# A two-layer graph network: exponentials of edge scores taken on ScalarE straight from a score row, weight sums and block ends moved from GpSimd to VectorE, and a new order of the first blocks

## The chip, the cores and the metric

The kernel runs on one NeuronCore of a Trainium2 chip. The metric is the device time of one execution in microseconds (us). Engines are called PE (TensorE), DVE (VectorE), ACT (ScalarE), POOL (GpSimd) and SP (SyncE, which only issues DMAs here).

## The reference

There are 1250 nodes with 1024 features and 41250 edges. The first layer normalises, runs a relational graph convolution with two relations, and adds its output back. The second layer is the one that the change touches:

```python
def _L1_gnn_ref(x, W, a, src, dst):
    h = x @ W                                    # 1250 x 1024 @ 1024 x 1024
    al, ar = h @ a[0, :d], h @ a[0, d:]
    e = jnp.exp(-jax.nn.leaky_relu(al[src] + ar[dst], negative_slope=0.1))
    rowsum = jax.ops.segment_sum(e, src, num_segments=N)
    h_prime = jax.ops.segment_sum(e[:, None] * h[dst], src, num_segments=N)
    return jax.nn.elu(h_prime / (rowsum[:, None] + 1e-5))

x = x + _L0_gnn_ref(relu(layernorm(x)), ...)
x = x + _L1_gnn_ref(relu(layernorm(x)), W, a, src, dst)
```

## The kernel before

Nodes are kept in T = 10 tiles of 128 (the last has 98). The edges have been turned into a dense matrix of counts between every two nodes, so the second layer is dense: the weight between source node i and destination node j is the count times exp of minus the leaky relu of the summed score. The scores are stored with their sign turned, so the weight before the count is the lesser of exp(z) and exp(0.1 z), where z is the score of i plus the score of j.

**The places where scores lie.** `scores(t)` (L871) copies the two scores of the nodes of tile t into `score`; `n_ar[:, t]` is then a column, one number for each partition (destination node). `row(t)` (L1037) turns the other score into a row that is the same in all partitions, `rows[:, t, :]`, by a PE transpose (L1040) and a DVE copy (L1041).

**One source tile s** (128 source nodes against all 10 tiles of destinations, 128 x 1280 numbers) goes through these steps:

- `add_scores(s)` (L1091, DVE): z = row + column, written by pieces of 4, 4 and 2 tiles (512, 512 and 256 columns).
- `exps(s)` (L1096 and L1097, ACT): exp(0.1 z) into a second buffer `tenth(s)`, exp(z) in place in `raw(s)`.
- `lesser(s)` (L1102, DVE), `times_counts(s)` (L1108, DVE): the lesser of the two, times the counts.
- `sum_weights(s)` (L1116 to L1128, POOL): adds the ten tiles into `zsum`, which `sum_rows(s)` (L1177, PE) sums over partitions; `inverse(s)` (L1182, L1183, DVE) follows.
- `high_parts(s)` (L1132, ACT), `low_parts(s)` (L1136, DVE), `differences(s)` (L1140, DVE): the weights split in a high and a low part h and l, and a combination m of both, so that three fast fp32r products give an fp32 product. The values of the nodes are split in the same way: `parts_of(t)` (L893 ACT, L894 DVE) and `third_form(engine, t)` (L1144).

**Blocks and their matmuls.** A block (s, c) is the 128 outputs of source tile s in half c of the 1024 columns. `multiply(s, c, "hl")` (L1165) is 20 matmuls of 512 columns; `scale(s, c)` (L1171, ACT) then multiplies the sum in PSUM by 4097; `multiply(s, c, "m")` is 10 more into the same sum. `elu_of(s, c)` (L1193 to L1196) and `put_out(s, c)` (L1201, L1202) scale by the inverse, apply the elu, add x, which `load_rest` (L1157) fetched, and store. The very last block uses `last_out` (L1209 to L1213) instead.

**Buffers.** For s of 2 and more, all s share one `raw` and one `tenth` buffer; h, l, m and `zsum` alternate between two sets. The weights of s = 0 and s = 1 for the first eight tiles of destinations (`exps(s, 0, T - 2)` and so on) are made early, while the last product of x and W (L986: seven half-size products for each pair of tiles, whose PSUM results ACT evacuates at L1001, L1012, L1023 and L1029) still runs. In that part the framework's scheduler chooses the order.

**Order.** From L1319 on, the order of PE, DVE, ACT and POOL is the order in which the program is written. A first part (L1322 to L1360) fills in the last two tiles (A = 8 to B = 10) of s = 0 and s = 1; six of the ten third forms are on POOL, four on DVE. Then the loop over s (L1362 to L1399) overlaps the products of s with making the weights of s + 1. In iteration s the PE runs (s, 0) "hl", (s-1, 1) "m", (s, 1) "hl" and (s, 0) "m": 60 matmuls.

Of the kernel before, what the change touches and what calls it, by code (L numbers as in the profile page):

```python
# [8 lines left out]
F32 = mybir.dt.float32  # L9
# [4 lines left out]
AF = mybir.ActivationFunctionType  # L14
ALU = mybir.AluOpType
# [12 lines left out]
T = 10  # L28
# [382 lines left out]
def fast_arm(tc, ctx, edges, firsts, w_root, conv_bias, wo, w_gat, a_gat, out,  # L411
# [443 lines left out]
    score = const.tile([128, 2, T], F32, name="score")  # L855
    nc.vector.memset(score, 0.0)
    n_al, n_ar = score[:, 0, :], score[:, 1, :]
    rows = meta[:, D + 2:D + 2 + T * 128].rearrange("p (t n) -> p t n", t=T)

    def three(name):  # L860
# [10 lines left out]
    def scores(t):  # L871

        n = ROWS[t]
        ends = hs[t].rearrange("p (h c) -> p h c", h=2)[:n, :, H]
        nc.vector.tensor_copy(score[:n, :, t], ends)

# [207 lines left out]
        for t0, t1 in zip(ends, ends[1:]):  # L1086
            yield t0, t1, [at(f, t0, t1) for f in forms]

    def add_scores(s, a=0, b=T):
        for t0, t1, (z,) in each(a, b, raw(s)):  # L1090
            nc.vector.tensor_tensor(z, rows[:, s:s + 1, :].to_broadcast([128, t1 - t0, 128]),  # L1091
                                    n_ar[:, t0:t1, None].to_broadcast([128, t1 - t0, 128]), ALU.add)

    def exps(s, a=0, b=T):
        for t0, t1, (z, y) in each(a, b, raw(s), tenth(s)):
            nc.scalar.activation(y, z, AF.Exp, scale=0.1)  # L1096
            nc.scalar.activation(z, z, AF.Exp)  # L1097

    def lesser(s, a=0, b=T):

# [6 lines left out]
            z = z.rearrange("p t (a j) -> p t a j", a=4)  # L1107
            nc.vector.tensor_tensor(z, z, counts[:, t0:t1], ALU.mult)  # L1108

    def sum_weights(s, first=True, rest=True):  # L1110

        z, total, add = raw(s), zsum[s % 2], nc.gpsimd.tensor_add
        if s < 2:
            if first:
                y = early[1].rearrange("p (t n) -> p t n", n=128)
                add(y[:, :4], at(z, 0, 4), at(z, 4, 8))  # L1116
                add(y[:, :2], y[:, :2], y[:, 2:4])
                add(total, y[:, 0], y[:, 1])
            if rest:
                for t in (8, 9):  # L1120
                    add(total, total, at(z, t, t + 1)[:, 0])
        else:
            y = by_dsts[s].bitcast(F32)[:, :HD].rearrange("p (t n) -> p t n", n=128)
            add(y[:, :4], z[0][2], z[1][2])  # L1124
            add(total, at(z, 8, 9)[:, 0], at(z, 9, 10)[:, 0])
            add(y[:, :2], y[:, :2], y[:, 2:4])
            add(y[:, 0], y[:, 0], y[:, 1])
            add(total, total, y[:, 0])  # L1128

    def high_parts(s, a=0, b=T):  # L1130
        for t0, t1, (z, h) in each(a, b, raw(s), sets[s % 2]["h"]):
# [51 lines left out]
        nc.vector.reciprocal(inv[:n], inv[:n])  # L1183

    def buffers(s, c):
        return ends[3 * c:3 * c + 3]

    def elu_of(s, c):

        n = ROWS[s]  # L1190
        r, e, x = (v[:n] for v in buffers(s, c))
        v = sums_of[s, c][:n]
        nc.scalar.activation(e, v, AF.Exp, scale=invs[s][:n])  # L1193
        nc.scalar.activation(e, e, AF.Relu, bias=one[:n], scale=-1.0)
        nc.gpsimd.tensor_tensor(e, x, e, ALU.subtract)  # L1195
        nc.scalar.activation(r, v, AF.Relu, scale=invs[s][:n])  # L1196

    def put_out(s, c):
        n = ROWS[s]
        r, e, x = (v[:n] for v in buffers(s, c))  # L1200
        nc.vector.tensor_add(e, e, r)  # L1201
        nc.sync.dma_start(out[s * 128:s * 128 + n, c * HD:c * HD + HD], e)  # L1202

    def last_out(s, c):

        n = ROWS[s]
        r, e, x = (v[:n] for v in buffers(s, c))
        v = sums_of[s, c][:n]
        nc.scalar.activation(e, v, AF.Exp, scale=invs[s][:n])  # L1209
        nc.vector.tensor_scalar(r, v, invs[s][:n], 0.0, op0=ALU.mult, op1=ALU.max)  # L1210
        nc.vector.scalar_tensor_tensor(r, x, -1.0, r, op0=ALU.add, op1=ALU.add)
        nc.vector.scalar_tensor_tensor(e, e, 1.0, r, op0=ALU.min, op1=ALU.add)
        nc.sync.dma_start(out[s * 128:s * 128 + n, c * HD:c * HD + HD], e)  # L1213

    os_, oTs, hTs = {}, {}, {}
# [63 lines left out]
    for (i, j), after in zip(order, order[1:] + [None]):  # L1279
        p2(i, j)  # L1280
        p6(i, j)
        if j == 1 and i + 1 < T // 2:
            norm(2 * i + 2)
            turn_first(i + 1)
            norm(2 * i + 3)
        p5(i, j)
        p7(i, j)
        if after:
            p1(*after)
            if j == 1:  # L1290
                turn_second(i + 1)
        p4(i, j)
        p3(i, j)
        if j == 1:
            if after:
                rest_of_pair(i + 1)
            if after:
                for t in (2 * i, 2 * i + 1):
                    scores(t)
                for t in range(0 if i == 1 else 2 * i, 2 * i + 2):  # L1300
                    parts_of(t)
                for t in range(0 if i == 1 else 2 * i, 2 * i + 2):
                    row(t)
            if i == T // 2 - 2:

                early += [big.tile([128, D + 2], F32, name="early", tag="x8")[:, :D], long_tile("early")[:, :D]]
                for s in range(2):
                    add_scores(s, 0, T - 2)
                    exps(s, 0, T - 2)
                    lesser(s, 0, T - 2)  # L1310
                    times_counts(s, 0, T - 2)
                    sum_weights(s, rest=False)
                    if s == 0:
                        high_parts(s, 0, T - 2)
                        low_parts(s, 0, T - 2)
# [3 lines left out]
    with tc.manual_schedule(  # L1319
            engines={mybir.EngineType.PE, mybir.EngineType.DVE, mybir.EngineType.Activation,  # L1320
                     mybir.EngineType.Pool}):
        for t in range(6):  # L1322
            third_form(nc.gpsimd, t)
        for c in range(2):
            open_block(0, c)
            load_rest(0, c)
        multiply(0, 0, "hl", 0, A)
        for t in (A, A + 1):
            scores(t)
        sets[1]["h"], sets[1]["l"] = [place(wide("zh", "wo4"))], [place(wide("zl", "h"))]  # L1330
        high_parts(1, 0, A)
        low_parts(1, 0, A)
        hhs[A] = work.tile([128, KD * 128], F32R, name="hh8", tag="hT", bufs=2)
        parts_of(A)
        hhs[A + 1] = big.tile([128, D + 2], F32R, name="hh9", tag="x9")
        parts_of(A + 1)
        multiply(0, 1, "hl", 0, A)
        for t in (A, A + 1):
            row(t)
        for s in range(2):  # L1340
            add_scores(s, A, B)
            exps(s, A, B)
        for s in range(2):
            lesser(s, A, B)
            times_counts(s, A, B)
            high_parts(s, A, B)
        for i in (1, 0):
            sets[i]["m"] = [place(work.tile([128, T * 128], F32R, name="zm", tag="z", bufs=2))]
        for s in range(2):
            low_parts(s, A, B)  # L1350
            sum_weights(s, first=False)
        hms[A] = work.tile([128, KD * 128], F32R, name="hm8", tag="hT", bufs=2)
        hms[A + 1] = big.tile([128, D + 2], F32R, name="hm9", tag="x8")
        differences(0)
        for t in range(6, T):
            third_form(nc.vector, t)
        open_block(1, 0)
        multiply(1, 0, "hl", 0, A)
        for s, c in ((0, 0), (0, 1), (1, 0)):
            multiply(s, c, "hl", A, B)  # L1360

        for s in range(T):  # L1362
            nxt = s + 1 if 2 <= s + 1 < T else None
            if s > 1:
                open_block(s, 0)
                multiply(s, 0, "hl")
            if s:
                scale(s - 1, 1)
            if nxt:
                add_scores(nxt)  # L1370
            if s:
                elu_of(s - 1, 0)
                load_rest(s, 0)
            if nxt:
                exps(nxt)
            if s > 1:
                put_out(s - 2, 1)
            if s:
                put_out(s - 1, 0)
            if nxt:  # L1380
                lesser(nxt)
                times_counts(nxt)
                sum_weights(nxt)
                high_parts(nxt)
            scale(s, 0)
            if nxt:
                low_parts(nxt)
            sum_rows(s)
            if s:
                multiply(s - 1, 1, "m")  # L1390
                open_block(s, 1)
                multiply(s, 1, "hl")
            multiply(s, 0, "m")
            inverse(s)
            if s:
                elu_of(s - 1, 1)
                load_rest(s, 1)
            if nxt or not s:
                differences(s + 1)  # L1399
        scale(T - 1, 1)  # L1400
        elu_of(T - 1, 0)
        multiply(T - 1, 1, "m")
        put_out(T - 2, 1)
        put_out(T - 1, 0)
        last_out(T - 1, 1)


@with_exitstack
# [149 lines left out]
```

## Time and profile before

| | before |
|---|---|
| time, median of 3 runs (lowest to highest) | 602.16 us (601.88 to 602.29) |
| time of the profiled execution | 602.22 us |
| its span, first to last instruction | 600.4 us |
| granted clock of the PE, mean of the span | 0.989 |
| busy: PE, DVE, ACT, POOL | 580.2, 429.7, 260.3, 120.7 us |
| start of (3, 0) "hl" on the PE | 489.55 us |
| last DMA issued (L1213) | 594.70 us |

Times in the profile are us from the start of the span. In a timeline, each line has the start, the time taken, the engine, the line of the kernel, the operation, its output and input, and how many were merged; the brackets give the idle time before it and who ended it. A wait is written as engine, line, the engine and line it waited for: sum in us, how often, the longest. In a chain of waits each line is the time at which a step of the chain starts and how long it lasts on the chain.

### The profile page before, as it was taken

Reading aid. Unit: us, or ns where it says so; the run is one execution under the profiler, and the core shown is the slowest. Engines: PE = TensorE matmul, PEld = TensorE weight load, DVE = VectorE, ACT = ScalarE, POOL = GpSimd, SP = SyncE. Lnnn points to the kernel's source line nnn. Section 1 sums busy time; section 2 is a strip of 40 time slices with the busy share of each in tenths; the row PEclk is TensorE's granted clock in tenths of the full one; section 3 lists DMA queues with packets and bytes.
Section 4 is the critical chain, followed back from the end, with each engine's and each line's share of the span. In section 5 each row is a group of like instructions: output and inputs, shape, how many; then the busy total and the mean of one; then the engine's idle time right before and its main releaser. Section 6 shows DMA issues by size and latency. Waiting matters only on the chain.

```text
span 600.4 us, 8407 instructions
## 1 busy us (share of the span) xinstructions
PE 580.2 (97%) x2848; PEld 420.9 (70%) x2848; DVE 429.7 (72%) x988; ACT 260.3 (43%) x516; POOL 120.7 (20%) x111
## 2 busy tenths in 40 slices
PE   8999999999999999999999999999996899999993
PEld 5666666666656767767766888888874788888872
DVE  5889887888772766469899734234669988888831
ACT  3666566665542000003412233324513866677632
POOL 5010000000000000000000000000293666667740
PEclk9999999999999999999999999999997999999997
DMA  8950111110108601100126700000000022222211
GB/s 282 345 138 2 37 35 37 35 29 7 29 0 258 197 37 55 51 36 36 70 86 186 219 10 1 0 2 1 18 19 0 35 87 84 90 91 71 71 66 64
DMA packets 21928, 43.80 MB, mean 73 GB/s; under 512 B 2638, under 2 KB 7886, under 8 KB 21876
## 3 DMA queue, kind: packets, MB, share of 16 engines
q1 hardware_dynamic: 20308, 38.05, 18.8%
q0 software_dynamic: 1424, 5.12, 4.5%
q8 instruction: 24, 0.39, 0.3%
q14 instruction: 28, 0.23, 0.1%
q10 hardware_dynamic: 144, 0.00, 0.0%
HBM read 24.53 MB, written 13.52 MB: 63 GB/s over the span
## 4 chain that ended last, share of the span: by engine, by line
PE 84%; DVE 5%; issue 5%; DMA 2%; ACT 2%; SPq 1%; POOL 0%; POOLq 0%; DVEq 0%; ACTq 0%
PE mm L721 17%; PE mm L986 12%; PE mm L798 12%; PE tp L1165 10%; PE mm L1165 7%; PE acc L521 7%; PE mm L844 6%; PE z L986 5%; PE mm L902 3%; DMA w<-in_w_cat_dram 2%; PE p L902 2%; PE tp L576 1%; DVE d L1091 1%; PE mm L845 1%; DVE hm L1144 1%
## 5 line engine op out<-in xcount | busy, mean ns | idle before, releaser
L721 PE MATMUL mm<-w,hT 128*128 128x429 f32 (+1 forms) x320 | 143.7, 535 | 1.2 <-DMA w<-in_w_cat_dram 1.1
L520 DVE TENSOR_SCALAR key<-meta 125x320 bf16<-125x320 f16 x330 | 85.1, 300 | 24.2 <-PE acc L521 12.2
L528 ACT ACTIVATE cnt<-acc 128x320 f32 x110 | 49.8, 453 | 70.0 <-PE acc L521 62.0
L521 PEld LDWEIGHTS <-lo 125*128 125x128 bf16 x330 | 40.5, 126 | 50.5 <-issue 36.8
L798 PE MATMUL mm<-y,cnt 128*128 128x286 bf16 (+3 forms) x600 | 75.2, 284 | 0.4 <-DVE y L614 0.4
L521 PE MATMUL acc<-key,lo 125*128 125x320 bf16 x330 | 72.2, 303 | 0.0
L798 PEld LDWEIGHTS <-cnt 128*128 128x128 f16 (+1 forms) x600 | 59.5, 99 | 14.7 <-issue 1.0
L721 PEld LDWEIGHTS mm<-w,hT 128*128 128x128 f32 (+1 forms) x320 | 51.4, 190 | 6.5 <-issue 5.1
L1116 POOL TENSOR_TENSOR early<-early 128x512 f32<-128x512 f32 x2 | 2.6, 1278 | 239.3 <-DVE early L1108 239.3
L986 PE MATMUL mm<-w,a 128*128 128x257 f32 (+3 forms) x192 | 44.9, 379 | 0.0
L986 PEld LDWEIGHTS mm<-w,a 128*128 128x128 f32 (+1 forms) x192 | 35.7, 187 | 5.8 <-ACT h L1012 0.4
L809 ACT ACTIVATE bias<-bias 128x286 f32<-128x286 f32 (+1 forms) x10 | 4.4, 442 | 80.2 <-DVE bias L808 80.2
L844 PE MATMUL mm<-wo,meta 128*128 128x512 f32 (+1 forms) x80 | 37.6, 592 | 0.0
L1165 PE MATMUL tp<-hm,zm 128*128 128x512 f32 (+1 forms) x120 | 30.3, 399 | 1.5 <-ACT tp L1171 1.5
L495 DVE TENSOR_TENSOR lo<-meta 125x768 bf16<-125x768 f16 x55 | 30.3, 551 | 0.1
L1091 DVE TENSOR_TENSOR d<-meta,score 128x512 f32<-128x512 f32 (+1 forms) x26 | 26.8, 1082 | 0.0
L1165 PEld LDWEIGHTS tp<-hm,zm 128*128 128x128 f32 (+1 forms) x120 | 21.6, 184 | 7.2 <-ACT tp L1171 1.9
L1124 POOL TENSOR_TENSOR d<-d,d 128x512 f32<-128x512 f32 x8 | 19.0, 2380 | 34.7 <-DVE d L1108 34.7
L587 POOL DMA_DIRECT2D x<-h x10 | 9.1, 909 | 83.7 <-ACT h L558 73.6
L1201 DVE TENSOR_TENSOR meta<-meta,d 128x512 f32<-128x512 f32 x9 | 12.7, 1410 | 16.7 <-POOL meta L1195 16.7
L1165 PE MATMUL tp<-hh,zh 128*128 128x512 f32 (+3 forms) x60 | 24.0, 401 | 0.0
L1165 PE MATMUL tp<-parts,zl 128*128 128x512 f32 (+3 forms) x60 | 23.9, 398 | 0.0
(213 smaller groups left out, 1143.5 us busy)
## 6 DMA issues: line engine op xcount, KB each, us to landing
x<-h POOLq DMA_DIRECT2D x9, 512.0 KB, 4.6
xd<-x SPq DMA_DIRECT2D x9, 512.0 KB, 2.6
x<-in_x_dram SPq DMA_DIRECT2D x8, 512.0 KB, 12.7
w<-in_L_gnn_W_dram SPq DMA_DIRECT2D x8, 512.0 KB, 7.5
w<-in_w_cat_dram SPq DMA_DIRECT2D x8, 429.0 KB, 10.3
squares<-cnt SPq DMA_DIRECT2D x10, 320.0 KB, 3.2
d<-squares SPq DMA_DIRECT2D x40, 80.0 KB, 2.0
d<-xd SPq DMA_DIRECT2D x9, 256.0 KB, 2.6
```

What stands on the lines that cost most here:

```text
L495: nc.vector.tensor_tensor(los[q // 2], iota_lo, lows[:, q:q + 2, :].rearrange("p q j -> p (q j)")[:, None, :].to_broadcast([PE_, 128, 2 * J]),
L520: nc.vector.tensor_scalar(key, iota_key, keys[:, q, j:j + 1], None, op0=ALU.is_equal)
L521: nc.tensor.matmul(acc[:, :2 * T * W], los[q // 2][:, :, (q % 2) * J + j], key, start=(j == 0), stop=(j == J - 1))
L528: nc.scalar.activation(cnt_w[:, :, bass.ds(b, W)], a3, AF.Copy)
L721: nc.tensor.matmul(pys[t][:ROWS[t], r, :F + HF], hTs[t][0][:, k, :ROWS[t]], wcat[k][:, r, :], start=(k == 0), stop=(k == KD - 1))
L798: nc.tensor.matmul(pm[:n, r, :f], cnt[:k, h, r, t * 128:t * 128 + n], ybs[h][:k, s, r, :f], start=(h == 0 and s == 0), stop=(h == T - 1 an ...
L844: nc.tensor.matmul(po[:n, c, :], oT[:, i, :n], wo_of[i][:, cs], start=(i == 0), stop=False)
L902: nc.tensor.matmul(o, hT[:, k, :n], wg[k][:, c0:c1], start=(k == 0), stop=(k == KD - 1))
L986: nc.tensor.matmul(o[:a.shape[2], :c1 - c0], a[:, k, :], b[k][:, c0:c1], start=(start and k == 0), stop=(k == KH - 1), skip_group_check=no ...
L1091: nc.vector.tensor_tensor(z, rows[:, s:s + 1, :].to_broadcast([128, t1 - t0, 128]), n_ar[:, t0:t1, None].to_broadcast([128, t1 - t0, 128]) ...
L1124: add(y[:, :4], z[0][2], z[1][2])
L1165: nc.tensor.matmul(sums_of[s, c][:n], at(sets[s % 2][f], t, t + 1)[:k, 0, :n], h[:k, c * HD:c * HD + HD], start=(t == 0 and f == "h"), sto ...
```

## The change

`add_scores` goes. `exps` reads the row itself and passes the column as the bias of the activation; a column serves one tile only, so each tile takes two instructions of 128 columns: exp(row + n_ar) and exp(0.1 row + tenths), where `tenths` is a new table with a tenth of `n_ar`, filled by one more small DVE instruction in `scores`. `sum_weights` becomes three or four DVE additions for each s; only the last two tiles of s = 0 and s = 1 are added on POOL (`sum_last`). `elu_of` loses its second Relu on ACT and its POOL subtraction; `put_out` takes two DVE instructions instead of one, and also serves the last block, whose x is loaded into another buffer. Two third forms stay on POOL, eight are on DVE. The first part and the first two turns of the loop are written out in a new order: all four blocks of s = 0 and 1 have their "hl" before `multiply(0, 0, "m")`, which follows the first `differences`. The loop starts at s = 2.

```diff
@@ scores
         nc.vector.tensor_copy(score[:n, :, t], ends)
+        nc.vector.tensor_scalar(tenths[:n, t:t + 1], ends[:, 1:2], 0.1, None, op0=ALU.mult)
@@ exps
-        for t0, t1, (z, y) in each(a, b, raw(s), tenth(s)):
-            nc.scalar.activation(y, z, AF.Exp, scale=0.1)
-            nc.scalar.activation(z, z, AF.Exp)
+        for t0, t1, forms in each(a, b, raw(s), tenth(s)):
+            for form, n, scale in zip(forms, (n_ar, tenths), (1.0, 0.1)):
+                for t in range(t0, t1):
+                    nc.scalar.activation(form[:, t - t0, :], rows[:, s, :], AF.Exp, bias=n[:, t:t + 1], scale=scale)
@@ sum_weights (the old body of POOL additions is removed)
+    def sum_weights(s):
+        z, y, add = raw(s), tenth(s)[0][2], nc.vector.tensor_add
+        n = T - 2 if s < 2 else T
+        add(y[:, :4], at(z, 0, 4), at(z, 4, 8))
+        if n == T:
+            add(y[:, :2], y[:, :2], at(z, 8, 10))
+        add(y[:, :2], y[:, :2], y[:, 2:4])
+        add(zsum[s % 2], y[:, 0], y[:, 1])
+    def sum_last(s):
+        for t in (T - 2, T - 1):
+            nc.gpsimd.tensor_add(zsum[s], zsum[s], at(raw(s), t, t + 1)[:, 0])
@@ buffers
-        return ends[3 * c:3 * c + 3]
+        r, e, x = ends[3 * c:3 * c + 3]
+        return r, e, slots[4][:, :HD] if (s, c) == (T - 1, 1) else x
@@ elu_of, put_out (last_out is removed)
         nc.scalar.activation(e, v, AF.Exp, scale=invs[s][:n])
-        nc.scalar.activation(e, e, AF.Relu, bias=one[:n], scale=-1.0)
-        nc.gpsimd.tensor_tensor(e, x, e, ALU.subtract)
         nc.scalar.activation(r, v, AF.Relu, scale=invs[s][:n])
...
-        nc.vector.tensor_add(e, e, r)
+        nc.vector.scalar_tensor_tensor(e, e, 1.0, x, op0=ALU.min, op1=ALU.add)
+        nc.vector.scalar_tensor_tensor(e, r, -1.0, e, op0=ALU.add, op1=ALU.add)
@@ the early weights of s = 0 and 1
-                    add_scores(s, 0, T - 2)
                     exps(s, 0, T - 2)
...
-                    sum_weights(s, rest=False)
+                    sum_weights(s)
@@ the first part, as it is after
+        for t in range(2):
+            third_form(nc.gpsimd, t)
         for c in range(2):
             open_block(0, c)
             load_rest(0, c)
         multiply(0, 0, "hl", 0, A)
         for t in (A, A + 1):
             scores(t)
...
+        for t in (A, A + 1):
+            row(t)
+        parts_of(A)
+        for s in range(2):
+            exps(s, A, B)
...
+        high_parts(1, 0, A)
+        multiply(0, 1, "hl", 0, A)
+        lesser(0, A, B)
+        times_counts(0, A, B)
+        high_parts(0, A, B)
+        low_parts(1, 0, A)
+        parts_of(A + 1)
+        low_parts(0, A, B)
+        lesser(1, A, B)
+        times_counts(1, A, B)
+        high_parts(1, A, B)
+        low_parts(1, A, B)
         open_block(1, 0)
         multiply(1, 0, "hl", 0, A)
         for s, c in ((0, 0), (0, 1), (1, 0)):
             multiply(s, c, "hl", A, B)
+        for s in range(2):
+            sum_last(s)
...
+        differences(0)
+        for t in range(2, T):
+            third_form(nc.vector, t)
+        exps(2)
+        for c in range(2):
+            scale(0, c)
+        scale(1, 0)
+        open_block(1, 1)
+        multiply(1, 1, "hl")
+        scale(1, 1)
+        differences(1)
+        sum_rows(0)
+        multiply(0, 0, "m")
+        inverse(0)
+        elu_of(0, 0)
+        multiply(0, 1, "m")
+        lesser(2)
+        times_counts(2)
+        high_parts(2)
+        low_parts(2)
+        elu_of(0, 1)
+        put_out(0, 0)
+        load_rest(1, 0)
+        sum_rows(1)
+        multiply(1, 0, "m")
+        inverse(1)
+        differences(2)
+        multiply(1, 1, "m")
@@ the loop, as it is after
+        for s in range(2, T):
+            more = s + 1 < T
+            open_block(s, 0)
+            multiply(s, 0, "hl")
+            if s > 2:
                 scale(s - 1, 1)
+            sum_weights(s)
+            elu_of(s - 1, 0)
+            if more:
+                exps(s + 1)
+            put_out(s - 2, 1)
+            load_rest(s - 1, 1)
+            put_out(s - 1, 0)
+            load_rest(s, 0)
+            if not more:
+                load_rest(s, 1)
+            if more:
+                lesser(s + 1)
+                times_counts(s + 1)
+                high_parts(s + 1)
             scale(s, 0)
+            if more:
+                low_parts(s + 1)
+            if s > 2:
+                multiply(s - 1, 1, "m")
+            open_block(s, 1)
+            multiply(s, 1, "hl")
             sum_rows(s)
             multiply(s, 0, "m")
+            if more:
+                differences(s + 1)
             inverse(s)
+            elu_of(s - 1, 1)
         scale(T - 1, 1)
         elu_of(T - 1, 0)
         multiply(T - 1, 1, "m")
         put_out(T - 2, 1)
         put_out(T - 1, 0)
-        last_out(T - 1, 1)
+        elu_of(T - 1, 1)
+        put_out(T - 1, 1)
```

More of the change, by code (lines that the diff above doesn't have):

```diff
@@ L857, in fast_arm @@
     n_al, n_ar = score[:, 0, :], score[:, 1, :]
+    tenths = const.tile([128, T], F32, name="tenths")
+    nc.vector.memset(tenths, 0.0)
     rows = meta[:, D + 2:D + 2 + T * 128].rearrange("p (t n) -> p t n", t=T)
@@ L1087, in each @@
             yield t0, t1, [at(f, t0, t1) for f in forms]
[L1089 to L1092, printed above, removed]
     def exps(s, a=0, b=T):
-        for t0, t1, (z, y) in each(a, b, raw(s), tenth(s)):
-            nc.scalar.activation(y, z, AF.Exp, scale=0.1)
-            nc.scalar.activation(z, z, AF.Exp)
+        for t0, t1, forms in each(a, b, raw(s), tenth(s)):
+            for form, n, scale in zip(forms, (n_ar, tenths), (1.0, 0.1)):
+                for t in range(t0, t1):
+                    nc.scalar.activation(form[:, t - t0, :], rows[:, s, :], AF.Exp, bias=n[:, t:t + 1], scale=scale)
     def lesser(s, a=0, b=T):
@@ L1108, in times_counts @@
             nc.vector.tensor_tensor(z, z, counts[:, t0:t1], ALU.mult)
[L1110 to L1128, printed above, removed]
+    def sum_weights(s):
[9 more added lines that the diff above has]
+            nc.gpsimd.tensor_add(zsum[s], zsum[s], at(raw(s), t, t + 1)[:, 0])
     def high_parts(s, a=0, b=T):
@@ L1200, in put_out @@
         r, e, x = (v[:n] for v in buffers(s, c))
[L1201 to L1212, printed above, removed]
+        nc.vector.scalar_tensor_tensor(e, e, 1.0, x, op0=ALU.min, op1=ALU.add)
+        nc.vector.scalar_tensor_tensor(e, r, -1.0, e, op0=ALU.add, op1=ALU.add)
         nc.sync.dma_start(out[s * 128:s * 128 + n, c * HD:c * HD + HD], e)
@@ L1321, in fast_arm @@
                      mybir.EngineType.Pool}):
-        for t in range(6):
+        for t in range(2):
             third_form(nc.gpsimd, t)
@@ L1329, in fast_arm @@
             scores(t)
+        hhs[A] = work.tile([128, KD * 128], F32R, name="hh8", tag="hT", bufs=2)
+        hhs[A + 1] = big.tile([128, D + 2], F32R, name="hh9", tag="x9")
+        for t in (A, A + 1):
[3 more added lines that the diff above has]
+            exps(s, A, B)
         sets[1]["h"], sets[1]["l"] = [place(wide("zh", "wo4"))], [place(wide("zl", "h"))]
         high_parts(1, 0, A)
+        multiply(0, 1, "hl", 0, A)
+        lesser(0, A, B)
+        times_counts(0, A, B)
+        high_parts(0, A, B)
         low_parts(1, 0, A)
-        hhs[A] = work.tile([128, KD * 128], F32R, name="hh8", tag="hT", bufs=2)
-        parts_of(A)
-        hhs[A + 1] = big.tile([128, D + 2], F32R, name="hh9", tag="x9")
         parts_of(A + 1)
[L1337 to L1356, printed above, removed]
+        low_parts(0, A, B)
[3 more added lines that the diff above has]
+        low_parts(1, A, B)
         open_block(1, 0)
@@ L1360, in fast_arm @@
             multiply(s, c, "hl", A, B)
[L1362 to L1367, printed above, removed]
-                scale(s - 1, 1)
[L1369 to L1384, printed above, removed]
-            scale(s, 0)
-            if nxt:
-                low_parts(nxt)
+        for s in range(2):
+            sum_last(s)
@@ new lines, in fast_arm @@
+        for i in (1, 0):
+            sets[i]["m"] = [place(work.tile([128, T * 128], F32R, name="zm", tag="z", bufs=2))]
+        hms[A] = work.tile([128, KD * 128], F32R, name="hm8", tag="hT", bufs=2)
+        hms[A + 1] = big.tile([128, D + 2], F32R, name="hm9", tag="x8")
+        differences(0)
[7 more added lines that the diff above has]
+        multiply(1, 1, "hl")
@@ L1388, in fast_arm @@
             sum_rows(s)
[L1389 to L1392, printed above, removed]
             multiply(s, 0, "m")
+            if more:
+                differences(s + 1)
             inverse(s)
[L1395 to L1399, printed above, removed]
+            elu_of(s - 1, 1)
         scale(T - 1, 1)
```

## The prediction

> **What bounds the kernel now.** I read the page first, then the waits of the PE after 410 us, then the windows around its gaps.
>
> ```profile
> PE 580.2 (97%) x2848; PEld 420.9 (70%) x2848; DVE 429.7 (72%) x988; ACT 260.3 (43%) x516; POOL 120.7 (20%) x111
> PE   8999999999999999999999999999996899999993
> PEclk9999999999999999999999999999997999999997
> ```
> ```profile
> PE mm L1165 <- ACT parts L1132: 5.6, 1, 5.6
> PE tp L1165 <- ACT tp L1171: 1.5, 1, 1.5
> PE mm L1165 <- DVE parts L1136: 0.5, 1, 0.5
> ```
> ```profile
> 449.85:455.64 5.79, 0.17 (x1) 0.00 (x0) 5.62 (x5) 2.01 (x5) 4.63 (x3) 0.87 0.00 0
> 455.64:461.41 5.77, 5.26 (x12) 3.81 (x13) 5.58 (x8) 1.58 (x3) 1.64 (x4) 0.54 0.00 0
> 471.30:472.97 1.67, 0.17 (x2) 0.01 (x1) 1.67 (x4) 1.67 (x5) 1.10 (x1) 1.00 0.00 0
> ```
>
> The PE is the bound almost everywhere; in the steady loop it never waits. What can be won lies in slices 31 and 32: a gap of 5.79 us, then 12 matmuls at a granted clock of 0.54 that take 5.77 us instead of 12 x 0.2325 = 2.79 (0.2325 is the usual step: 40 matmuls in 9.3 us), then a gap of 1.67. Together 10.4 us. The chain of waits says who is late:
>
> ```profile
> 439.85 3.91 DVE score L875 x2
> 443.76 1.13 DVE zl L1136
> 444.89 1.15 DVE parts L894
> 446.06 1.07 ACT hh L893
> 449.29 0.48 DVE meta L1041 x2
> 449.76 4.59 DVE d L1091 x2
> 457.41 1.74 DVE zm L1140
> 459.15 4.54 DVE hm L1144 x4
> ```
>
> It is DVE, in program order. Two copies of two columns take 3.91 us and two additions of 256 columns 4.59 us (the same form takes 0.41 elsewhere): POOL runs its third forms (L1144) at that time, and DVE waits for it. The end of the kernel is the other place:
>
> ```profile
> 591.87 0.69 DVE L1201 TENSOR_TENSOR d<-d,d 98x512 f32<-98x512 f32 x1 [6.27 <-POOL d L1195]
> 592.48 0.74 DVE L1210 TENSOR_SCALAR d<-tp,inv 98x512 f32<-98x512 f32 x1
> 593.26 0.69 DVE L1211 SCALAR_TENSOR_TENSOR d<-meta,d 98x512 f32<-98x512 f32 x1
> 593.98 0.69 DVE L1212 SCALAR_TENSOR_TENSOR meta<-meta,d 98x512 f32<-98x512 f32 x1
> ```
>
> The last matmul ends near 591.2; POOL's subtraction holds DVE until 591.87.
>
> **The price of one small exp.** No row has a 128-column exp with a bias column. The nearest:
>
> ```profile
> 7.66 2.17 ACT L583 ACTIVATE hT<-tp,lnw 128x128 f32<-128x128 f32 x8
> 476.32 0.72 ACT L1194 ACTIVATE d<-d,one 128x512 f32<-128x512 f32 x1
> 476.95 0.67 ACT L1196 ACTIVATE d<-tp,inv 128x512 f32<-128x512 f32 x1
> ```
>
> L583 has 128 columns and a scale column: eight in 2.17 us, one 0.37 long, so (2.17 - 0.37)/7 = 0.26 each. L1194 has a bias column and 512 columns: the next starts 0.63 later; less 384 columns at 0.832 ns (from 1058 ns at 1024 and 632 at 512) that is 0.31. I take p = 0.28, bounds 0.26 and 0.31; 20 of them are 5.6 us (5.1 to 6.2) against 3.28 for the six of before (491.68 to 494.96).
>
> **The steady loop, s = 3 on.** Per s, ACT loses two L1194 (1.26 us) and gains 2.3 in exps: 9.3 busy becomes 10.4 of 14.1, beside the PE. DVE loses `add_scores` (2.7) and gains 1.5 (sum of weights: 0.6 + 0.33 + 0.33 + 0.25) and 1.25 (two more instructions in `put_out`): no change. POOL's work goes, so its transfers of time to DVE go too (L1201 1.77 becomes 0.69). What matters is the chain inside a turn. Let (s, 0) "hl" start at 0: `elu_of(s-1, 0)` on ACT starts at 0.2 and its two instructions end their turn at 1.37 (two steps of 0.57 to 0.6); 20 exps follow; the last `lesser` comes 0.12 later; from it to the end of `scale(s, 0)` is 3.08 (496.97 to 500.05 before). So scale ends at 4.57 + 20p = 10.2 (9.8 to 10.8). The PE wants it for (s, 0) "m" at 11.9 (501.43 - 489.55). It holds, by 1.1 to 2.1 us. Exps also overwrite what `sum_weights(s)` reads: DVE ends low parts 0.4 after scale, then 1.45 + 0.3 + 1.5 gives 13.9, before the next turn's exps at 15.5. So the loop stays at 14.1 us per turn: the exps cost nothing there, hidden by 60 matmuls. On SP each `load_rest` now stands behind a `put_out`; four issues of 0.35 a turn, and x lands 2.6 us later (page) for use a turn on: nothing.
>
> **The first blocks.** This is where the time goes. PE: (0, 0) "hl" for eight tiles ends at 442.2 as before, transposes 442.4. The four score instructions now meet POOL only until its second third form ends, about 439.8 (two of 2.4 from 434.9, when the last matmul that reads w0 to w3 is done). DVE: row copies to 442.9; low part of tile 8, 1.15; lesser and counts, 0.82; low part of s = 1, 1.15; low part of tile 9 waits for ACT. ACT: hh of tile 8 (1.06) to 440.9, eight exps 443.3, high part 444.4, a short one after DVE 445.3, hh of tile 9 446.4. DVE then 447.55; three of 0.41, 448.8; ACT 0.45; low part 449.7; differences 1.4, 451.1; eight third forms at 1.14, 460.2. The PE has 77 matmuls left from 439.2 (13 of (0, 0), 32, 12, 20 of (1, 1)), 17.9 us, and reaches "m" of (0, 0) at 457.3, where it waits only for the last third form: it ends at 460.5, and three more "m" end at 467.5. `sum_last` on POOL, behind its two third forms, waits for the counts of s = 1 (448.8) and takes two additions of 0.52; `exps(2)`, which overwrite what it reads, start at 450 and end at 455.6. The three scales behind them on ACT are done by 457.4: hidden.
>
> DVE goes on from 460.2: differences 1.4, inverse 0.3, lesser and counts of s = 2 3.1, low parts 1.6 (466.6, just ahead of (2, 0) at 467.5), `put_out` 1.25, inverse 0.3, differences 1.4, `sum_weights(2)` 1.5: 471.1. Only then may ACT write the exps of s = 3: 476.7 (476.2 to 477.3), and 3.2 to the end of `scale(2, 0)`: 479.9 (479.4 to 480.5). The PE ended (2, 1) "hl" at 476.8 and waits: a new gap of 3.1 us (2.6 to 3.7), since no "m" lies between there. Then 2.33: (3, 0) starts at 482.3 instead of 489.55, with the same work left. Gain 7.2 us (6.7 to 7.8).
>
> **The end.** With the last matmul at E: exp at E + 0.15 takes 0.69, then two DVE instructions at 0.72 (the Relu on ACT runs beside the first): DMA issued at E + 2.3 instead of E + 3.5. DVE is free by then: `put_out(9, 0)` ends before E. Gain 1.2 us. What follows the last issue (5.7 us) stays.
>
> **What I hold back.** (a) 32 early exps of 128 columns take ACT 9.0 us instead of 4.2, between evacuations that the seven products wait for. One evacuation takes 0.39 of the 0.86 us that four matmuls beside it last, so 0.47 is spare: 0 where the order fits, 2.6 us where four of the eight evacuations stand behind four exps each (1.12 - 0.47); I take 0.5. (b) Scores or sums that meet POOL after all: at most the 3.91 of before less 2.3 that DVE waits for the PE there, 0 to 1.6; I take 0.5. Before 439.8 DVE's early work for s = 1 ends at 438.4 to 440, so the same cushion takes it. Ten instructions for `tenths` at 0.12 to 0.16 (L875's shortest and median) lie in DVE's idle time.
>
> Sum against the profiled execution: 602.22 - 7.2 - 1.2 + 1.0 = 594.8 us (span 593.0 + 1.82 around it). The median, 602.16, is 0.06 from it.
>
> **The clock.** The new gap of 3.1 us lies between two rows: 1.67 us left the clock at 1.00, 5.79 brought 0.54 and cost 5.77 - 2.79 = 3.0 us of slow matmuls. So it costs 0 to 3.0; I take 0, as it is nearer to the short one. The Trainium skill (TensorE: Matmul & The Clock Gate, Part 1) says that the array falls to half its clock after an idle window of about 3.4 us, and that the window runs freely. The two gaps of this trace agree with that. By its rule a gap at the upper bound, 3.7, would pay and the sum would be 597.8; one of 3.1 would not.
>
> **Rivals.**
>
> *Half the gain* (0.18): the clock drops in the new gap (3.0) or the early part loses its 2.6 us, or both: 597 to 600.4. For it: the gap is near. Against: DVE's rows are well known.
>
> *The products wait* (0.07): each of eight evacuations stands behind four exps, 1.1 us, 0.65 over what is spare: 5.2 us, and (b) at its bound: 601.1, no difference. Against: before, exps of 1.06 us stand there without a gap on the PE.
>
> *ACT becomes the bound of the loop, slower* (0.07): if small exps do not overlap, p = 0.72 - 0.32 = 0.40. From p = 0.366 (4.57 + 20p = 11.9) scale comes too late and each of six turns grows by 20(p - 0.366); the gap at s = 2 grows by 20(p - 0.28). The gain of 7.4 is gone near p = 0.405, where 2.5 + 6 x 0.78 = 7.2; a waiting time of 0.045 on top of each, p = 0.45, costs 3.4 + 10.1 and makes 608.3. Against it: L583 overlaps.
>
> *POOL is not gone*: two third forms and four additions are left. If the two still meet the scores, (b) is paid, no more; it is in the first two cases.
>
> **How the numbers follow.** My forecast, 592.5 to 597, has 0.63; half the gain 0.18; products 0.07; ACT 0.07; 0.05 for better than 592.5, if exps of s = 3 cost less wait. A measurement of this kernel can tell 0.2%, 1.2 us. Faster: 0.63 + 0.18 + 0.05, and some of the products' case, 0.87; same 0.05; slower 0.08. The range, 592.0 to 600.4, leaves out the two last rivals and the best end.
>
> **What would show it.** In the profile after: no wait of the PE on L1132 near 450; third forms on DVE in a row of eight, and "m" of (0, 0) after them; one gap on `scale` before (2, 0) "m", about 3 us; (3, 0) near 482; turns of 14.1 us with no wait on scale; 128-column exps 0.28 apart; the last DMA 2.3 us after the last matmul. Wrong would be exps over 0.36 apart, a PE wait in each turn, or waits of L986 on ACT between 415 and 440.

## Result and the profile after

The changed kernel takes 597.04 us, median of 4 runs (596.75 to 597.24), beside 602.22 us for the kernel before (601.88 to 603.53) on the same chip: ratio 0.991, 95% interval 0.9892 to 0.9927. Its profiled execution took 597.06 us, span 595.3. The forecast was 594.8 with a range of 592.0 to 600.4: faster, as forecast, but 2.2 us short of it.

First the page of the kernel after (busy time, then two of the rows in 40 slices), and its waits of the PE from 405 us on (total, times, longest).

```profile
PE 578.6 (97%) x2848; PEld 420.6 (71%) x2848; DVE 416.5 (70%) x1031; ACT 276.0 (46%) x642; POOL 28.0 (5%) x42
PE   7999999999999999999999999999999979999994
PEclk9999999999999999999999999999999989999998
```
```profile
PE tp L1159 <- ACT tp L1165: 3.7, 1, 3.7
PE mm L1159 <- DVE hm L1138: 0.6, 1, 0.6
```

POOL's busy time falls from 120.7 to 28.0. The dip in slices 31 and 32 is gone in its old form, and so is the wait of 5.6 us on a high part. The wait of 1.5 us on scale has become one of 3.7 (L1165, in s = 2), which is now the only dip between the first slice and the last, in slice 33. The windows around it (PE, PEld, DVE, ACT, POOL busy; granted clock; DMA) show what that costs:

```profile
477.73:481.57 3.84, 0.14 (x3) 0.05 (x1) 3.36 (x8) 2.69 (x8) 0.00 (x0) 0.95 0.02 7
481.57:485.36 3.79, 3.79 (x11) 3.04 (x12) 3.48 (x7) 1.62 (x3) 0.00 (x0) 0.60 0.00 0
485.36:499.58 14.22, 14.22 (x63) 11.51 (x62) 10.92 (x20) 10.92 (x29) 0.00 (x0) 1.00 0.21 75
```

The first row is a gap of 3.84 us; behind it ten "m" matmuls run at clock 0.60 and last 3.79 instead of 2.33: 1.46 more. The third row is the first turn of the steady loop, with no idle PE. (3, 0) starts at 485.36; it was 489.55 before. The chain of waits of the kernel after says why (start, us, what):

```profile
451.64 9.09 DVE hm L1138 x8
460.73 1.40 DVE zm L1134
...
468.36 2.76 DMA out_dram<-d
...
471.22 0.07 ACT d L1187
...
471.81 0.68 ACT d L1188
472.49 5.87 ACT d L1097 x20
```

The eight third forms stand in a row and end at 460.73 (forecast 460.2). Behind them is a link that the forecast has not: the store of block (0, 0), issued at 468.36. The Exp of `elu_of(1, 0)` (L1187) writes the buffer that this store reads, so ACT sits idle for 3.9 us until 471.2, and the 20 exps stand behind it in ACT's order. (The dots stand for pieces left out.)

At the end, these lines of the timeline (DVE, then SP's queue) answer to the four shown of before:

```profile
587.92 0.69 DVE L1194 SCALAR_TENSOR_TENSOR meta<-meta,d 98x512 f32<-98x512 f32 x1 [0.82 <-ACT meta L1187]
588.72 0.69 DVE L1195 SCALAR_TENSOR_TENSOR meta<-d,meta 98x512 f32<-98x512 f32 x1
```
```profile
589.44 0.34 SPq L1196 DMA_DIRECT2D out_dram<-meta  x1
```

The last matmul ends at 587.16, the last DMA is issued 2.3 us later; before it was 591.31 and 594.70, 3.4 later. So 4.2 us were won up to (3, 0) and 1.1 at the end, 5.3 together; the loop and the stretch behind the last issue take 0.2 more than before, and the span fell by 5.1 (600.4 to 595.3). These are single executions: at the start of the program, which the change does not touch, the PE waits 1.9 us for the DMA of `w_cat` in the one after and 1.1 in the one before, so the split is good to about 1 us, not to a tenth.

### The profile page after: what moved, and what is told of

It is laid out like the page before. It is cut to its first block, busy times and chain, and to the rows that moved or that the text cites. A ratio compares the mean times of both kernels' runs of the same rounds, so it can differ in the third digit from the quotient of the medians.

```text
span 595.3 us, 8473 instructions
## 1 busy us (share of the span) xinstructions
PE 578.6 (97%) x2848; PEld 420.6 (71%) x2848; DVE 416.5 (70%) x1031; ACT 276.0 (46%) x642; POOL 28.0 (5%) x42
## 4 chain that ended last, share of the span: by engine, by line
PE 80%; DVE 11%; issue 3%; DMA 2%; ACT 2%; SPq 1%; POOL 0%; ACTq 0%; DVEq 0%; POOLq 0%
PE mm L721 17%; PE mm L798 12%; PE mm L989 11%; PE tp L1159 11%; PE acc L521 7%; PE mm L1159 7%; PE mm L844 5%; PE z L989 5%; DVE cnt L1051 2%; DMA w<-in_w_cat_dram 2%; DVE hm L1138 2%; PE tp L576 1%; DVE cnt L1049 1%; ACT d L1097 1%; PE mm L845 1%
## 5 line engine op out<-in xcount | busy, mean ns | idle before, releaser
L1159 PE MATMUL tp<-hm,zm 128*128 128x512 f32 (+1 forms) x120 | 31.5, 413 | 3.7 <-ACT tp L1165 3.7
L1097 ACT ACTIVATE d<-meta,tenths 128x128 f32<-128x128 f32 x84 | 27.3, 395 | 0.0
L1097 ACT ACTIVATE d<-meta,score 128x128 f32<-128x128 f32 x84 | 27.3, 395 | 0.0
L1159 PE MATMUL tp<-hh,parts 128*128 128x512 f32 (+1 forms) x60 | 23.7, 394 | 0.0
L1159 PE MATMUL tp<-parts 128*128 128x512 f32 (+1 forms) x60 | 23.6, 393 | 0.0
L844 PEld LDWEIGHTS mm<-wo,meta 128*128 128x128 f32 (+1 forms) x80 | 14.4, 187 | 12.9 <-issue 12.1
## 6 DMA issues: line engine op xcount, KB each, us to landing
w<-in_w_cat_dram SPq DMA_DIRECT2D x8, 429.0 KB, 10.4
```

What stands on the lines that cost most here:

```text
L844: nc.tensor.matmul(po[:n, c, :], oT[:, i, :n], wo_of[i][:, cs], start=(i == 0), stop=False)
L1097: nc.scalar.activation(form[:, t - t0, :], rows[:, s, :], AF.Exp, bias=n[:, t:t + 1], scale=scale)
L1159: nc.tensor.matmul(sums_of[s, c][:n], at(sets[s % 2][f], t, t + 1)[:k, 0, :n], h[:k, c * HD:c * HD + HD], start=(t == 0 and f == "h"), sto ...
```

## Experiments

Theory: DVE, held up by POOL's third forms, set the first blocks; the change won by taking four third forms off POOL and by giving the PE four blocks of "hl" to do meanwhile, and lost some of it to the new gap and its clock. Rival: the gain comes from the form of the exps and of the sums, in every turn. Times of the kernel before on the chip of each group: 602.40 (e1 to e4), 602.25 (e5 to e8), 602.82 (e9 to e11).

### What held DVE: e1 and e2

e1 puts the four third forms back on POOL in the changed kernel.

```diff
-        for t in range(2):
+        for t in range(6):
             third_form(nc.gpsimd, t)
...
-        for t in range(2, T):
+        for t in range(6, T):
             third_form(nc.vector, t)
```

> The kernel after, but with six third forms on POOL and four on DVE, as before the change. Theory (the first blocks were late because DVE's short instructions wait for POOL while it runs third forms): four third forms less on DVE save 4 x 1.14 = 4.6 us, but the scores take near 3.9 us again instead of 0.35, of which the wait for the row transposes hides 1.8, and the ten short DVE instructions between 442 and 450 us wait too, 3 to 5 us; so no gain, 596 to 600 us, with score copies of 1 to 2.5 us each in the trace. Rival (the new order of the blocks alone did it, sharing costs little): the chain on DVE gets 4.6 us shorter, and the time is 592 to 593 us.

Measured 598.81 us (596.99 to 599.19), ratio 0.9932 (0.991 to 0.9954). DVE's timeline in e1 shows the scores waiting for POOL again:

```profile
439.79 1.18 DVE L877 COPY score<-h 128x2 f32<-128x2 f32 x1
440.94 2.33 DVE L877 COPY score<-h 98x2 f32<-98x2 f32 x1
```

In the kernel after the same two copies last 0.17 and 0.16. But only four third forms are then left on DVE:

```profile
456.20 4.62 DVE L1138 TENSOR_TENSOR hm<-parts,hh 128x1024 fp32r<-128x1024 f32 x4
```

They end at 460.7, as the eight do in the kernel after: for DVE the two choices come out even. The PE loses 1.6 us at a transpose behind the scores and 3.3 at a low part, and less than the kernel after at `scale`:

```profile
PE tp L1159 <- DVE zl L1130: 3.3, 1, 3.3
PE tp L1043 <- DVE tenths L878: 1.6, 1, 1.6
PE tp L1159 <- ACT tp L1165: 1.4, 1, 1.4
```

In all, e1 is 1.8 us slower than the kernel after, and still 3.6 faster than the kernel before in its group (602.40).

e2 moves the same four third forms in the kernel before, and nothing else.

```diff
-        for t in range(6):
+        for t in range(2):
             third_form(nc.gpsimd, t)
...
-        for t in range(6, T):
+        for t in range(2, T):
             third_form(nc.vector, t)
```

> The kernel before, with one part of the change alone: two third forms on POOL and eight on DVE. Theory (sharing with POOL made DVE late): the scores fall from 3.91 to about 0.4 us and the two short additions from 4.59 to 0.8, so the chain up to the first differences gets 7 us shorter, and the gap of 5.79 us at 450 us and its slow clock go; but eight third forms stand between the differences, +4.6 us, and the PE has only three blocks of hl ahead, so a new gap opens before the first m; net 2 to 4 us faster, 598 to 600 us. Rival (sharing costs little, the order matters): the four third forms add 4.6 us, 605 to 607 us.

Measured 601.17 us (600.89 to 603.76, 10 runs), ratio 0.9985 (0.9975 to 0.9996): 1.2 us and no more, short of the 2 to 4 expected. The gap of 5.79 us is gone, as the theory has it. Yet with only three blocks ahead the PE reaches "m" long before the third forms are done and takes each as DVE ends it, one per 1.14 us. The waits and two windows of e2:

```profile
PE mm L1165 <- DVE hm L1144: 3.1, 7, 0.6
```
```profile
454.00:463.00 9.00, 5.88 (x12) 2.35 (x11) 8.96 (x11) 0.00 (x0) 0.00 (x0) 0.66 0.00 0
463.30:467.50 4.20, 4.20 (x12) 3.33 (x12) 4.20 (x6) 3.98 (x7) 1.59 (x1) 0.55 0.04 7
```

Twelve matmuls in 9.0 us let the clock fall to 0.66, and the next twelve run at 0.55. So relief of POOL's third forms is worth 1.2 us in the old order and some 1.8 in the new one (e1), about a third of the gain at most: the forms moved to DVE take their own time there. Most of the gain, 3.6 us, comes with the rest of the change: the new order with its fourth block ahead, the direct exps and sums, and the ends. No run changes the order alone.

### The new gap and its clock: e3, e9, e4

e3 fills the gap of the kernel after with 14 matmuls of 512 columns into a half bank that nobody reads; they add nothing to the output.

```diff
             sum_rows(s)
+            if s == 2:
+                for _ in range(14):
+                    nc.tensor.matmul(spare_of[2, 1], at(sets[0]["h"], 0, 1)[:, 0, :], hhs[0][:, :HD],
+                                     start=True, stop=True, skip_group_check=True)
             multiply(s, 0, "m")
```

> The kernel after, with 14 idle matmuls of 512 columns on the PE (3.26 us, into a half bank that nobody reads) in the gap before (2, 0) m. Theory (the ten matmuls after the gap take 3.79 instead of 2.33 us because the gap of 3.84 us lets the clock fall): the ten take 2.33 us again, the granted clock stays at 1.0, and the time falls by 1.3 to 1.5 us to 595.6. Rival (they are slow because of what they read, or the wait on their input): no change, 597.0, the ten still near 3.8 us.

Measured 595.23 us (595.09 to 596.10), ratio 0.9879 (0.9863 to 0.9896). PE's timeline in e3:

```profile
477.82 3.50 PE L1404 MATMUL mm<-hh,parts 128*128 128x512 f32 x14
481.59 2.61 PE L1162 MATMUL tp<-hm,zm 128*128 128x512 f32 x10 [0.26 <-ACT tp L1168]
```

The useful ten in the chain of waits of the kernel after:

```profile
481.57 3.94 PE tp L1159 x10
```

They start at the same moment in both and last 2.61 instead of 3.94. So the clock was a cost of its own.

e9 moves `elu_of(1, 0)` behind exps(3), so that these no longer stand behind the wait for the store.

```diff
-            elu_of(s - 1, 0)
+            if s > 2:
+                elu_of(s - 1, 0)
             if more:
                 exps(s + 1)
+            if s == 2:
+                elu_of(1, 0)
...
-            put_out(s - 1, 0)
-            load_rest(s, 0)
+            if s > 2:
+                put_out(s - 1, 0)
+                load_rest(s, 0)
...
                 low_parts(s + 1)
+            if s == 2:
+                put_out(1, 0)
+                load_rest(2, 0)
```

> The kernel after, with only elu and output of (1, 0) moved behind the exps of s = 3 (the sums of s = 2 stay where they are). Theory (before these exps ACT waits until 471.2 us for the output of (0, 0) to leave the buffer that elu of (1, 0) overwrites, and takes 1.2 us for that elu; the first exps themselves need only the first addition of the sums, done at 470.6): exps from 470.6 instead of 472.4, scale(2, 0) near 479.8, gap 2.1 instead of 3.8 us; and as a gap of 2.1 does not lower the clock, another 1.4 to 1.5 us: 593.9 us (593.4 to 594.6). Rival (any gap over two microseconds lowers it here): 595.3.

Measured 594.57 us (593.46 to 594.72), ratio 0.9855 (0.9836 to 0.9874). ACT's and PE's timelines in e9:

```profile
470.36 1.28 ACT L1097 ACTIVATE d<-meta,score 128x128 f32<-128x128 f32 x4 [3.37 <-DVE d L1114]
```
```profile
479.64 2.60 PE L1159 MATMUL tp<-hm,zm 128*128 128x512 f32 x10 [2.08 <-ACT tp L1165]
```

The exps now begin as the *first* addition of the sums (L1114) ends, at 470.36 instead of 472.38. These two microseconds were the store's: in the kernel after the inverse that `elu_of(1, 0)` needs was ready at 468.60, so its 1.2 us would have fitted in ahead of that addition's end. The first four exps need only the first addition; the next four overwrite the buffer in which the sums are formed, and in e9 the sums end (471.58) just before these four start (471.62). The gap shrinks to 2.08, and the clock stayed at 1.00.

e4 goes further: the sums of s = 2 and exps(3) already beside block (0, 1), ahead of (1, 0)'s end.

```diff
         low_parts(2)
+        sum_weights(2)
         elu_of(0, 1)
+        exps(3)
         put_out(0, 0)
...
-            sum_weights(s)
+            if s > 2:
+                sum_weights(s)
             elu_of(s - 1, 0)
-            if more:
+            if more and s > 2:
                 exps(s + 1)
...
```

`put_out(1, 0)` and `load_rest(2, 0)` go behind `low_parts(3)` as in e9.

> The kernel after, with the sums of weights of s = 2 right behind its low parts, the exps of s = 3 right behind them on ACT, and elu and output of (1, 0) behind the weights of s = 3. Theory (the gap at s = 2 is the chain sums, DMA wait of (1, 0), exps, lesser, counts, high parts, scale; 4.4 us of it is only order): sums end near 468.5 instead of 471.9, exps near 474.4 instead of 478.4, scale(2, 0) near 477.6, where the PE arrives at 477.7; the gap of 3.84 us and 1.46 us of slow clock go; (3, 0) starts near 480.4 instead of 485.4 and the time is 592.0 (591.5 to 593). Rival (the loop behind is bound by ACT and DVE too, and gives the time back): (3, 0) starts earlier, but waits on scale appear in the next turns and the time stays above 595.

Measured 592.41 us (591.76 to 592.58), ratio 0.9831 (0.9815 to 0.9848). The exps start at 467.43, the gap is gone; the PE's waits are 0.6 and 0.5.

### The exps in the steady loop: e10, e5, e11

e10 does the exps of the last two tiles twice from s = 4 on, four more a turn.

```diff
+        if s > 3:
+            for t0, t1, forms in each(8, T, raw(s), tenth(s)):
+                for form, n, scale in zip(forms, (n_ar, tenths), (1.0, 0.1)):
+                    for t in range(t0, t1):
+                        nc.scalar.activation(form[:, t - t0, :], rows[:, s, :], AF.Exp, bias=n[:, t:t + 1], scale=scale)
```

> The kernel after, with the four exps of the last two tiles done twice (same output) in each turn from s = 4 on. Theory (cover of 1.3 us in a turn): four more take 4 x 0.293 = 1.17 us, up to 1.3 if a repeat waits for the write before it; scale ends just before the PE wants it: 597.0 us (596.7 to 598). Rival (ACT's time is on the path in each turn already): 6 x 1.17 = 7.0 us more, 604.

Measured 596.30 us (596.05 to 598.33), ratio 0.9899 (0.9874 to 0.9924). All waits of the PE in e10 from 405 us on:

```profile
PE tp L1164 <- ACT tp L1170: 3.6, 1, 3.6
PE mm L1164 <- DVE hm L1143: 0.6, 1, 0.6
```

Both lie ahead of the loop's steady part: four more are covered.

e5 does ten of them twice, each directly behind the first.

```diff
                     nc.scalar.activation(form[:, t - t0, :], rows[:, s, :], AF.Exp, bias=n[:, t:t + 1], scale=scale)
+                    if s > 3 and t < 5:
+                        nc.scalar.activation(form[:, t - t0, :], rows[:, s, :], AF.Exp, bias=n[:, t:t + 1], scale=scale)
```

> The kernel after, with ten of the twenty exps done twice (same output) in each turn of the loop from s = 4 on, six turns. Theory (the exps in the loop cost nothing because scale(s, 0) ends 10.5 us after the start of (s, 0) hl and the PE wants it at 11.8; the cover is 1.3 us): ten more take 10 x 0.293 = 2.93 us, scale comes at 13.4, the PE waits 1.6 us on it in each of six turns, 9.8 us in all: 606.8 us (605 to 608.5), turns of 15.8 instead of 14.2. Rival (ACT has 3.3 us idle in a turn, so the loop takes them): 597 to 598 us.

Measured 619.50 us (617.60 to 620.49), ratio 1.028 (1.0253 to 1.0307): slower as the theory had it, but by far more. ACT's timeline in e5:

```profile
486.51 0.40 ACT L1097 ACTIVATE d<-meta,score 128x128 f32<-128x128 f32 x1
486.94 0.40 ACT L1099 ACTIVATE d<-meta,score 128x128 f32<-128x128 f32 x1
487.24 0.39 ACT L1097 ACTIVATE d<-meta,score 128x128 f32<-128x128 f32 x1
```

A repeat into the same destination starts 0.43 us after the first, the next exp 0.30 after that; 30 exps take 10.2 us instead of 5.87. That is 4.3 more, less a cover of 1.3 makes 3.0, and the six turns wait 2.2 to 3.0 each, 16.9 in all. Of the rest of the 22.5 us over the kernel after, most is clock. PE's timeline in e5, two of the six gaps:

```profile
518.09 4.14 PE L1161 MATMUL tp<-hm,zm 128*128 128x512 f32 x10 [2.21 <-ACT tp L1167]
536.90 2.61 PE L1161 MATMUL mm<-hm,zm 128*128 128x512 f32 x10 [2.89 <-ACT mm L1167]
```

After the shorter gap ten matmuls take 4.14 us, after the longer one 2.61. Three of the six gaps (2.91, 2.21, 2.96) were paid for in clock, three (2.89, 2.96, 2.90) were not: between 2.2 and 3.0 us it is not length that decides.

e11 gives the loop its old form of exps back from s = 4 (sums of scores on DVE, wide exps); DVE is then 12.1 and ACT 8.1 of 14 us busy.

```diff
+    direct = exps
+    def exps(s, a=0, b=T):
+        if s < 4:
+            return direct(s, a, b)
+        for t0, t1, (z,) in each(a, b, raw(s)):
+            nc.vector.tensor_tensor(z, rows[:, s:s + 1, :].to_broadcast([128, t1 - t0, 128]),
+                                    n_ar[:, t0:t1, None].to_broadcast([128, t1 - t0, 128]), ALU.add)
+        for t0, t1, (z, y) in each(a, b, raw(s), tenth(s)):
+            nc.scalar.activation(y, z, AF.Exp, scale=0.1)
+            nc.scalar.activation(z, z, AF.Exp)
```

> The kernel after, with row plus column on DVE and wide exps from s = 4 on only. Theory (in the loop the form of the exps is off the path): DVE gets 1.6 us more (three additions) and ACT 2.6 less in a turn, the PE's turn stays at 14.2 us: 597.0 us (596.6 to 597.6). Rival (DVE becomes late for the next turn's sums, or the direct form was worth time in each turn): over 599.

Measured 596.80 us (595.90 to 597.85), ratio 0.9893 (0.9875 to 0.9911): as the kernel after. In the loop the form of the exps is off the path; the rival falls.

### The other two parts: e7 and e6

e7 has the old form of the exps everywhere, the first blocks too (the last six lines of e11's edit as the body of `exps`).

> The kernel after, with row plus column added on DVE first and the exps in two wide instructions on each piece, as before the change. Theory (the direct form pays where DVE is the bound, before s = 3, and nowhere else): two short additions between 442 and 450 us, +0.4 to 0.8, and 2.7 us for s = 2 on DVE's chain ahead of (2, 0) hl with the exps behind them, +2 to 4 us; the loop stays at 14.2 a turn; 599 to 601.5 us. Rival (20 exps of 0.293 cost more than they save, as ACT is in the chain before the gap at s = 2): 594 to 596.5 us.

Measured 605.96 us (604.65 to 607.33), ratio 1.0067 (1.0046 to 1.0087): worse than both theories. ACT's timeline and PE's waits in e7:

```profile
465.48 0.63 ACT L1097 ACTIVATE d<-d 128x512 f32<-128x512 f32 x1 [11.84 <-DVE d L1094]
```
```profile
PE mm L1160 <- ACT mm L1166: 5.5, 1, 5.5
PE z L989 <- DVE h L1027: 2.3, 1, 2.3
```

exps(2) now need additions that stand on DVE behind the eight third forms, so ACT waits 11.8 us, and the scales behind it on ACT hold the first "m" back by 5.5. Earlier, two small additions of the early sums run into POOL's third forms (2.48 and 2.31 us instead of 0.42 and 0.29), and a product waits 2.3. So in this order the direct exps are needed, not for being cheap but for needing nothing from DVE while DVE is late. An order made for the additions, with the scales ahead of exps(2), was not tried.

e6 gives the ends of blocks their old form: second Relu on ACT, subtraction on POOL, `last_out` for the last block.

```diff
         nc.scalar.activation(e, v, AF.Exp, scale=invs[s][:n])
+        nc.scalar.activation(e, e, AF.Relu, bias=one[:n], scale=-1.0)
+        nc.gpsimd.tensor_tensor(e, x, e, ALU.subtract)
...
-        nc.vector.scalar_tensor_tensor(e, e, 1.0, x, op0=ALU.min, op1=ALU.add)
-        nc.vector.scalar_tensor_tensor(e, r, -1.0, e, op0=ALU.add, op1=ALU.add)
+        nc.vector.tensor_add(e, e, r)
...
-        elu_of(T - 1, 1)
-        put_out(T - 1, 1)
+        last_out(T - 1, 1)
```

> The kernel after, with the ends of blocks as before the change: second Relu on ACT, subtraction on POOL, one addition on DVE, and the last block as before. Theory (moving the ends won only the wait of DVE for POOL behind the last matmul): last DMA issued 3.5 us after the last matmul instead of 2.3, the loop still covered by the PE: 598.2 us (597.5 to 599.5). Rival (POOL's part in the ends made DVE late in the first blocks as well): over 600 us.

Measured 599.04 us (598.51 to 600.20), ratio 0.9951 (0.9933 to 0.9968). The last DMA is issued at 591.03, 3.4 us after the last matmul (587.64): 1.1 us of the loss of 2.0. The wait in s = 2 grows from 3.7 to 4.2; the rest stays open.

### A better one: e8

e8 is e4 with three third forms on POOL instead of two (`range(3)` and `range(3, T)` in e1's places), which takes the 0.6 us wait on DVE's row of third forms.

> The kernel with sums and exps of s = 3 ahead (592.4), with three third forms on POOL instead of two. Theory (DVE's chain from 442.6 to the last third form still holds the PE 0.6 us, and scale(2, 0) 0.5): POOL ends at 441.8, within the time in which DVE waits for the row transposes anyway; 1.14 us less on DVE, both small gaps go: 591.3 us (591.0 to 591.8). Rival (the third one meets scores and first parts of tile 8 and makes them later by as much): 592.4 or above.

Measured 591.44 us (591.21 to 592.01), ratio 0.9821 (0.9805 to 0.9838), twice the gain of the change. After 405 us the PE waits once, 0.2 us, for scale.

## Why the prediction was right, and where it was short

**Range and point.** The measured 597.04 lies in the range because the range took in the case "half the gain" (597 to 600.4, chance 0.18); it is just outside the forecast proper (592.5 to 597, chance 0.63).

**The first blocks: their times right, POOL's part too large.** All three parts of the 10.4 us went, and DVE kept to its forecast: third forms in a row of eight ending at 460.73 (460.2), row copies to 443.07 (442.9), first "m" waiting 0.6 for the last of them. That DVE was late is shown; that POOL made it so holds for single instructions (the scores), but taking the third forms off POOL gave only 1.2 to 1.8 us (e2, e1). How the rest divides between the order and the direct exps stays open.

**The price of an exp: right.** Four in 1.27 us, one 0.395 long, so (1.27 - 0.395)/3 = 0.29 each; 20 take 5.87 (forecast 5.6, bounds 5.1 to 6.2).

**The steady loop: right.** Turns are 14.2 us with the PE always busy. `scale(3, 0)` ends 10.5 after the turn's start (forecast 10.2), wanted at 11.8: a cover of 1.3, which e10 and e5 confirm from its two sides.

**The end: right.** 1.1 us (1.2).

**What was held back: not needed.** The four score instructions take 0.35 us from 440.61, when POOL's two third forms have ended (439.43); no product waits for an early exp. Nearly all of the 1.0 us was still there. This is in part chance: a longer wait for `w_cat` (0.8 us) and three matmuls more of (0, 0) done before 438 us (0.7) happened to cancel.

**The new gap: its place right, its size short.** Forecast: PE there at 476.8, `scale` done at 479.9, gap 3.1. Measured: 477.73, 481.53 and 3.84. Of the PE's 0.93, 0.5 came in with the end of the third forms. The step that failed for `scale` is "only then may ACT write the exps of s = 3": it took exps(3) to wait for the end of the sums. The first of them wait only for the first addition, which would have let them start near 470.4 (e9), but `elu_of(1, 0)` ahead of them waited for a store's 2.76 us, which the forecast had not followed, and they started at 472.38. The two errors partly cancel, and the forecast looks better than its step.

**The clock: wrong.** Its cost was taken at 0, because a gap of 3.1 is nearer to 1.67 us than to 5.79; it cost 1.46 (e3, with the gap filled, does the ten in 1.33 less by its row). Then 0.93 + 0.74 + 1.46 = 3.1 us of lateness of (3, 0), less the 1.0 held back: about the 2.2 that the forecast was short. Of the case "half the gain" one half came true: the clock fell, at half the price given there (1.46 of 3.0), and the early part lost nothing. The rule of the Trainium skill (TensorE: Matmul & The Clock Gate, Part 1), an idle window of about 3.4 us that runs freely, agrees with the gap of 3.84 and with 1.67 and 2.08. It does not agree with e5: no idle window of 3.4 us fits into a gap of 2.21 us, which was enough, while 2.96 sometimes was not. Here the measurement decides.

**Rivals.** ACT as the bound needed 0.366 per exp, 7.3 us of exps a turn. Measured exps plus cover are 5.87 + 1.3 = 7.2, so the bound was well placed, and e5, at 10.2, shows that past it the loop does slow; at 0.29 the exps stayed under it. The products did not wait.

## What to carry to other kernels

When a pass goes to another engine, follow the order of that engine's queue: what stands behind an operand that comes late costs more than the instructions themselves, as e7 and the store in front of exps(3) show, while the steady loop did not feel the change at all. Work taken off one engine takes time on the next: a helper that slows its neighbour's short instructions may still be worth about as much as it costs (e1, e2, and the third form given back to POOL in e8). When a change has several parts, undo each alone, and from both sides where it can be done, before saying which one won. For each instruction that rewrites a buffer, ask which store or reader of it was issued last, and when that ends.

## What was not expected of the hardware

- A copy of two columns on DVE takes 0.17 us alone and 1.18 to 2.33 us (e1) beside POOL's operations on 128x1024 (2.35 us each in the kernel after): a tiny instruction can wait for about a whole one of POOL's.
- Counted as the PE's idle time alone, the granted clock fell after gaps of 2.21, 2.91, 2.96 and 3.7 us and stayed after others of 1.50 (the 1.67 of before), 2.08, 2.89, 2.90 and 2.96. The price differs too: after the gap at s = 2, hardly changed at 3.6 us in e10 and e11, the ten matmuls took 4.00 and 4.63 us beside 3.94. It may be the moment at which a gap falls that decides, as with a freely running window; no run moved one gap alone, so that stays open. Twelve matmuls spread over 9 us lowered it as well (e2).
- An exp that repeats the one just before it, same input and same output, starts 0.43 us after it instead of 0.29 (e5).
